# Graph convolution and mixture of experts on one core: blocks of 896 edges, the first norm on ScalarE, and a fixed order ahead of the gathers

## The chip, the core and the metric

The kernel runs on one core of one Trainium2 chip. The metric is device time in microseconds of one execution. Medians over several executions are compared; a profiled execution gives the trace. TensorE does matrix products, VectorE and ScalarE elementwise work[...], and SyncE (SP) and ScalarE issue plain transfers.

## The reference

`x` has 6250 rows of 256 numbers, and 106250 directed edges `src -> dst` are sorted by `dst`. Cut to what matters:

```python
def layernorm(x): return (x - mean(x)) / sqrt(var(x) + 1e-5)

def gnn(f, src, dst, W, b):
    ns = rsqrt(max(count(src), 1)); nd = rsqrt(max(count(dst), 1))
    msg = (f @ W)[src] * ns[src][:, None]
    return relu(segment_sum(msg, dst) * nd[:, None] + b)

def ffn(x):                       # 8 experts, hidden size 1024
    p = softmax(x @ Wr + br)      # the two best experts per row, weights renormed
    xn = layernorm(x)
    return sum over the 2 experts e of
        w_e * (gelu((xn * ln_g[e] + ln_b[e]) @ W1[e] + b1[e]) @ W2[e] + b2[e])

x = x + gnn(layernorm(x), src, dst, W, b)
x = x + ffn(layernorm(x))
```

## The kernel before

All work is in one function, `gnn_then_moe`. It has two stages, and the second interleaves three streams.

**Stage one, ahead of the gathers.** Rows are handled as 49 tiles of 128 (`NT`), in 7 groups of 7 (`NG`, `GT`). The stage prepares three things.

- *The counts of the source nodes.* Each index is split into its lower 7 bits and the rest (L272 to L278, `lo` and `hi`). The 831 columns of indices (`NCH`) go in 26 chunks of 32 (`GC`). For a chunk, function `count` compares the digits with a ramp on VectorE, giving two one-hot tensors, `oh_lo` (L340, 128x4096) and `oh_hi` (L345, 128x1568). TensorE then sums 32 products of them into `hist` (L350). The target nodes are counted in the same way into `hist_d`.
- *The edge blocks.* An edge list is laid out as rows of `BE` = 768 edges (`CE` = 6 columns of 128), 139 rows, so two partition groups (128 rows and 11). TensorE turns them so that an edge column lies along the partitions: `srcT` holds the sources, `relT` the targets relative to the block's window of 64 nodes (`WIN`). VectorE works out the windows, and counts the strays, the edges that fall outside; with none, a branch (L396) skips a repair part.
- *The table* `ytab` in HBM. A row is the normed row of `x` times `ns`, split into three bf16 pieces (`NPC`) whose sum is the fp32 value. The statistics come from VectorE (`stats`, L143 and L144). Per group VectorE makes `y` (L380), ScalarE rounds it to piece 1 (L385), VectorE subtracts (L386), ScalarE rounds piece 2 (L387), VectorE subtracts to piece 3 (L388), and SP stores the group (L389, 1344 KB). The tiles `y` and `yb` have two buffers each.

**Stage two.** A loop over the blocks, `for b in range(NBE)`. Per block POOL issues one indirect gather per column (L909, 128 table rows into `msg`, with `3 * CE` buffers), VectorE makes the one-hot `oh` of the targets (L915), TensorE sums the messages per node of the window (`pm`, L924), and VectorE adds this to `accT` at the window's place (L930). Beside the first 17 blocks (`HISTB`) go the chunks of `hist_d` that are not counted yet. When the last block that can touch a tile has gone (`CLOSE`), `tile_sums` makes its rows; after 9, 17, 25, 33, 40, 45 and 49 tiles `route_group` picks experts and POOL scatters the rows by expert (L688). Expert steps (`expert_step`, 56 of 256 rows, L845 and L858) run between the blocks, and POOL adds their results to the output (L867).

**Order.** The instructions of each engine come from a scheduler that may move work ahead of its place in the program. In the kernel before it puts 11 of the 26 chunks of `hist_d` among the work of stage one, ahead of the first gather. Each engine then runs its list strictly in order, and waits on semaphores.

Of the kernel before, what the change touches and what calls it, by code (L numbers as in the profile page):

```python
# [17 lines left out]
P = 128  # L18
# [4 lines left out]
def gnn_then_moe(  # L23
# [34 lines left out]
    CE = 6  # L58
# [3 lines left out]
    NCOL = NBE * CE  # L62
    WIN = 64
# [82 lines left out]

# [3 lines left out]
    NR = (P, NBE - P)  # L150
    dst_f = [early.tile([n, BE], F32, name=f"dst_f{h}") for h, n in enumerate(NR)]
    bad = [early.tile([n, BE], F32, name=f"bad{h}") for h, n in enumerate(NR)]
    flag_i = early.tile([1, 1], I32, name="flag_i")
    lo = {n: hl.tile([P, NCH], BF16, name=f"{n}_lo") for n in ("src", "dst")}
# [7 lines left out]
    scale = early.tile([P, NT], F32, name="scale")  # L162
    mv = early.tile([P, NT, 2], F32, name="mv")

    with tc.tile_pool(name="rows", bufs=1) as rows, tc.tile_pool(
        name="rowsp", bufs=2, space=PSUM
    ) as rowsp:
        flat = {}
        rows_i = {}
        for name, v, pad in (("src", src, 0), ("dst", dst, NOWHERE)):  # L170
            f = rows.tile([P, NCH], I32, name=f"{name}_flat")
            nc.vector.memset(f[:, FULL:NCH], NPAD - 1)
            b = rows.tile([NR[1], BE], I32, name=f"{name}_b")
            nc.vector.memset(b, pad)
            a = rows.tile([P, BE], I32, name=f"{name}_a")
            flat[name] = f
            rows_i[name] = (a, b)

        for name, v in (("src", src), ("dst", dst)):
            f, (a, b) = flat[name], rows_i[name]  # L180
            nc.sync.dma_start(f[:, :FULL], v[: FULL * P].rearrange("(p c) -> p c", p=P))
            if REST:
                nc.sync.dma_start(
                    f[:REST, FULL:NCH], v[FULL * P :].rearrange("(p c) -> p c", c=1)
                )
            nc.scalar.dma_start(a, v[: P * BE].rearrange("(p c) -> p c", p=P))
            nc.scalar.dma_start(
                b[: NR[1] - 1, :],
                v[P * BE : (NBE - 1) * BE].rearrange("(p c) -> p c", c=BE),
            )  # L190
            nc.scalar.dma_start(
                b[NR[1] - 1 : NR[1], :LASTE],
                v[(NBE - 1) * BE :].rearrange("(p c) -> p c", p=1),
            )

# [7 lines left out]
        for r0, r1 in ((0, split), (split, LASTROWS)):  # L203
# [3 lines left out]
        nc.scalar.dma_start(gw_sb, gnn_w.rearrange("(k p) d -> p k d", p=P))  # L207
        nc.scalar.dma_start(wr_sb, wr.rearrange("(k p) e -> p k e", p=P))
        nc.scalar.dma_start(b2_sb, b2)
        nc.scalar.dma_start(  # L210
            gb_sb, bass.AP(tensor=gnn_b.tensor, offset=gnn_b.offset, ap=[[0, P], [1, D]])
        )
        nc.scalar.dma_start(
# [3 lines left out]
        ident = const.tile([P, P], F32, name="ident")  # L217
        make_identity(nc, ident)
# [4 lines left out]
        nc.gpsimd.memset(accT, 0.0)  # L223
        nc.gpsimd.iota(iota_w, pattern=[[0, CE], [1, WIN]], base=0, channel_multiplier=0,
                       allow_small_or_imprecise_dtypes=True)
        ones = const.tile([P, P], F32, name="ones")
        nc.vector.memset(ones, 1.0)
# [6 lines left out]
        pcol = const.tile([P, 1], F32, name="pcol")  # L234
        nc.gpsimd.iota(pcol, pattern=[[0, 1]], base=0, channel_multiplier=1,
                       allow_small_or_imprecise_dtypes=True)
        eps = const.tile([P, 1], F32, name="eps")
        nc.vector.memset(eps, EPS)
        dump_xs = const.tile([P, 2], F32, name="dump_xs")
        dump_out = const.tile([P, 2], F32, name="dump_out")  # L240
        for s in range(2):
            nc.vector.tensor_scalar(
                dump_xs[:, s : s + 1], pcol, float(GONE + s * P), None, op0=ALU.add
            )
            nc.vector.tensor_scalar(
                dump_out[:, s : s + 1], pcol, float(N + 1 + s * P), None, op0=ALU.add
            )
# [12 lines left out]
        zeros = const.tile([P, SB * XW], F32, name="zeros")  # L260
        nc.vector.memset(zeros, 0.0)
        valid = const.tile([P, 1], F32, name="valid")
        nc.vector.tensor_scalar(valid, pcol, float(LASTROWS), None, op0=ALU.is_lt)

        accf = accT.rearrange("p k n -> p (k n)")
# [4 lines left out]
        for name in ("src", "dst"):  # L270
            part_i = rows.tile([P, NCH], I32, tag="part_i", name="part_i")
            nc.vector.tensor_scalar(part_i, flat[name], P - 1, None, op0=ALU.bitwise_and)  # L272
            nc.vector.tensor_copy(lo[name], part_i)
            part_j = rows.tile([P, NCH], I32, tag="part_i", name="part_j")
            nc.vector.tensor_scalar(
                part_j, flat[name], 7, None, op0=ALU.logical_shift_right
            )
            nc.vector.tensor_copy(hi[name], part_j)  # L278


        strays = rows.tile([P, 2, 2], F32, name="strays")
        nc.vector.memset(strays, 0.0)
        wrow = rowsp.tile([1, 2, P], F32, tag="wrow", name="wrow")
        for h in range(2):
            n = NR[h]
            s_f = rows.tile([n, BE], F32, tag="s_f", name="s_f")
            nc.gpsimd.tensor_copy(s_f, rows_i["src"][h])
            nc.gpsimd.tensor_copy(dst_f[h], rows_i["dst"][h])
            w_f = rows.tile([n, 1], F32, tag="w_f", name="w_f")
            nc.vector.tensor_scalar(  # L290
                w_f, dst_f[h][:, 0:1], float(NPAD - WIN), None, op0=ALU.min
            )
            rel = rows.tile([n, BE], F32, tag="rel", name="rel")
            nc.vector.tensor_scalar(rel, dst_f[h], w_f, None, op0=ALU.subtract)

            early_b = rows.tile([n, 1], F32, tag="early_b", name="early_b")
            nc.vector.tensor_scalar(
                early_b, pcol[:n], STEPN, STEPN * h * P - SLACK, op0=ALU.mult, op1=ALU.add
            )
            real = rows.tile([n, BE], F32, tag="real", name="real")  # L300
            nc.vector.tensor_scalar(
                real, dst_f[h], early_b, -100000.0, op0=ALU.is_lt, op1=ALU.mult
            )
            nc.vector.tensor_tensor(rel, rel, real, ALU.add)
            nc.vector.tensor_scalar(real, dst_f[h], 0.0, None, op0=ALU.is_ge)
            nc.vector.scalar_tensor_tensor(
                bad[h], rel, 0.0, real, op0=ALU.is_lt, op1=ALU.mult,
                accum_out=strays[:n, h, 0:1],
            )
            nc.vector.scalar_tensor_tensor(  # L310
                real, rel, float(WIN), real, op0=ALU.is_ge, op1=ALU.mult,
                accum_out=strays[:n, h, 1:2],
            )
            nc.vector.tensor_tensor(bad[h], bad[h], real, ALU.add)
            nc.tensor.transpose(wrow[:, h, :n], w_f, ident[:n, :n])
            nc.vector.tensor_copy(win_i[:, h * P : h * P + n], wrow[:, h, :n])
            b0 = h * P
            for v, vT in ((s_f, srcT), (rel, relT)):
                vT3 = vT.rearrange("p (b j) -> p j b", j=CE)
                for j0 in range(0, CE, 3):  # L320
                    pt = rowsp.tile([P, 3, P], F32, tag="ptE", name="ptE")
                    for j in range(j0, j0 + 3):
                        nc.tensor.transpose(
                            pt[:, j - j0, :n], v[:, j * P : (j + 1) * P], ident[:n, :n]
                        )
                    nc.vector.tensor_copy(
                        vT3[:, j0 : j0 + 3, b0 : b0 + n], pt[:, :, :n]
                    )
        total = rowsp.tile([P, 4], F32, tag="total", name="total")
        nc.tensor.matmul(  # L330
            total, ones, strays.rearrange("p a b -> p (a b)"), start=True, stop=True
        )
        flag_f = rows.tile([P, 1], F32, name="flag_f")
        nc.vector.tensor_reduce(flag_f, total, AX.X, ALU.add)
        nc.vector.tensor_copy(flag_i, flag_f[0:1, :])

    def count(pool, hist, name, c0):
        n = min(GC, NCH - c0)
        oh_lo = pool.tile([P, P, GC], BF16, tag="oh_lo", name="oh_lo")
        nc.vector.tensor_tensor(  # L340
            oh_lo[:, :, :n], iota_lo[:, :, :n],
            lo[name][:, None, c0 : c0 + n].to_broadcast([P, P, n]), ALU.is_equal,
        )
        oh_hi = pool.tile([P, NT, GC], BF16, tag="oh_hi", name="oh_hi")
        nc.vector.tensor_tensor(  # L345
# [10 lines left out]
    with tc.tile_pool(name="s1o", bufs=2) as s1o, tc.tile_pool(  # L356
# [4 lines left out]
        for g in range(NG):  # L361
            upto = (g + 1) * len(starts) // NG
            for c0 in starts[done:upto]:
                count(s1o, hist, "src", c0)
# [667 lines left out]
```

## Time and profile before

| what | value |
|---|---|
| median of 3 runs | 2113.53 us (2109.73 to 2114.85) |
| the profiled execution | 2114.36 us |
| its span on the core | 2112.4 us |
| first gather starts | 226.2 us into the span |
| first scatter by expert (L688) | 520.5 us |
| POOL busy, whole span | 1130.6 us (54%) |
| VectorE busy, whole span | 722.1 us (34%) |
| ScalarE busy, whole span | 328.3 us (16%) |

The span is what the trace covers; the 2.0 us between it and the profiled execution's own time lie around it. A row of the profile such as `L340 DVE TENSOR_TENSOR oh_lo<-iota_lo,src_lo 128x4096` names line, engine (DVE is VectorE, ACT ScalarE, PE TensorE), operation, result and inputs, then the count, the busy time, the mean ns of one, and the idle time of the engine just before with what ended it. In the page's strip of 40 slices one slice is 52.8 us, and a digit is the busy share in tenths.

### The profile page before, as it was taken

The numbers are of one execution on the slowest core, as the hardware profiler recorded it, in microseconds if no ns is written. First come the engines' busy times: TensorE is split into PE (matmuls) and PEld (weight loads), VectorE is DVE, ScalarE is ACT, GpSimd is POOL, SyncE is SP. The second block draws the span as 40 slices with busy tenths as digits, with TensorE's granted clock in tenths as the row PEclk, the third lists the DMA queues.
The fourth block names the chain that finished last, engine by engine and source line by source line (L and its number), as shares of the span: only waits on it lengthen the run. The fifth ranks groups of instructions, "written<-read, shape, count | busy, mean of one in ns | idle before, by whom it ended". The sixth has DMA issues, their size and how long they took to land.

```text
span 2112.4 us, 28889 instructions
## 1 busy us (share of the span) xinstructions
PE 1506.4 (71%) x11167; PEld 1236.4 (59%) x11167; DVE 722.1 (34%) x2078; ACT 328.3 (16%) x671; POOL 1130.6 (54%) x1065
## 2 busy tenths in 40 slices
PE   2872655656544659865899559985698678699998
PEld 1872544534433448754687437864487467488886
DVE  9999533324111412223222232323213422211111
ACT  0004000002100212112112022211121113122222
POOL 4000577777577756777377772777547731221222
PEclk9999999955655569975899659995699589799999
DMA  5004344556355567856577565865676653655654
GB/s 167 1 1 154 121 134 131 159 162 198 100 161 159 164 201 255 256 151 201 188 245 235 151 197 189 276 191 153 217 221 186 202 164 102 210 173 177 187 166 108
DMA packets 127309, 359.70 MB, mean 170 GB/s; under 512 B 21060, under 2 KB 75148, under 8 KB 120000
## 3 DMA queue, kind: packets, MB, share of 16 engines
q0 software_dynamic: 74208, 191.76, 33.6%
q1 hardware_dynamic: 51780, 164.79, 22.1%
q8 instruction: 89, 1.46, 0.3%
q10 hardware_dynamic: 1180, 1.26, 0.2%
q14 instruction: 52, 0.43, 0.1%
HBM read 311.58 MB, written 46.16 MB: 169 GB/s over the span
## 4 chain that ended last, share of the span: by engine, by line
PE 42%; DMA 23%; issue 10%; POOL 9%; DVE 3%; ACT 2%; SPq 0%; POOLq 0%; DVEq 0%; ACTq 0%
DMA msg<-ytab,srcT 17%; PE py L858 16%; PE ph L845 15%; POOL msg L909 6%; PE pm L924 5%; DMA xin<-xs 4%; POOL xs L688 2%; DMA xs<-rowt,pos_i 1%; PE pa L528 1%; PE pa L780 1%; PE pb L571 1%; DMA out_x<-yo,to_i 1%; PE ptf L829 1%; DVE yo L863 1%; PE pb L566 1%
## 5 line engine op out<-in xcount | busy, mean ns | idle before, releaser
L909 POOL DMA_INDIRECT msg<-ytab,srcT x834 | 833.2, 999 | 516.4 <-DVE oh L915 193.4
L924 PE MATMUL pm<-oh,msg 128*128 128x64 bf16 x5004 | 308.2, 219 | 292.9 <-DMA msg<-ytab,srcT 279.3
L924 PEld LDWEIGHTS <-msg 128*128 128x128 bf16 x5004 | 250.9, 114 | 368.8 <-DMA msg<-ytab,srcT 338.3
L858 PE MATMUL py<-w,hT 128*128 128x256 f32 x1792 | 421.0, 389 | 16.6 <-DVE yo L863 14.1
L845 PE MATMUL ph<-xeT,w 128*128 128x256 f32 x1792 | 412.6, 387 | 2.6 <-ACT hT L849 1.4
L867 POOL DMA_INDIRECT out_x<-yo,to_i x112 | 178.9, 1597 | 407.9 <-DVE yo L863 379.5
L858 PEld LDWEIGHTS py<-w,hT 128*128 128x128 f32 x1792 | 342.5, 194 | 70.2 <-DVE yo L863 23.3
L845 PEld LDWEIGHTS ph<-xeT,w 128*128 128x128 f32 x1792 | 327.7, 193 | 66.1 <-ACT hT L849 7.3
L849 ACT ACTIVATE hT<-ph,w 128x256 f32<-128x256 f32 x448 | 210.9, 473 | 759.6 <-PE ph L845 754.6
L350 PEld LDWEIGHTS <-oh_lo 128*128 128x128 bf16 x1662 | 164.8, 150 | 64.9 <-issue 55.8
L930 DVE TENSOR_TENSOR accT<-accT,pm 128x128 f32 x139 | 39.6, 285 | 344.6 <-PE pm L924 343.8
L812 DVE SCALAR_TENSOR_TENSOR to<-xin,dump_out 128x2 f32<-128x2 f32 x56 | 8.9, 159 | 415.4 <-DMA xin<-xs 415.4
L863 DVE TENSOR_SCALAR yo<-py,gate 128x256 f32<-128x256 f32 x112 | 54.1, 483 | 267.4 <-PE py L858 267.3
L350 PE MATMUL hist_d<-oh_hi,oh_lo 128*128 128x49 bf16 x831 | 89.4, 277 | 47.5 <-DVE oh_hi L345 47.0
L688 POOL DMA_INDIRECT xs<-rowt,pos_i x98 | 94.7, 966 | 41.9 <-issue 27.2
L528 PE MATMUL pa<-gw_sb,accT 128*128 128x256 f32 x196 | 73.5, 511 | 36.8 <-DVE keep L782 32.9
L350 PE MATMUL hist<-oh_hi,oh_lo 128*128 128x49 bf16 x831 | 84.7, 278 | 14.2 <-DVE oh_hi L345 13.6
L915 DVE TENSOR_TENSOR oh<-iota_w,relT 128x384 bf16<-128x384 bf16 x139 | 76.5, 554 | 26.5 <-PE pm L924 14.3
L829 PE MATMUL ptf<-ident,xin 128*128 128x128 f32 x224 | 37.9, 294 | 63.4 <-DMA xin<-xs 63.4
L780 PE MATMUL pa<-b_sb,wT 8*128 8x256 f32 x98 | 59.5, 708 | 26.7 <-DVE keep L782 23.2
L528 PEld LDWEIGHTS pa<-gw_sb,accT 128*128 128x128 f32 x196 | 45.1, 251 | 48.6 <-DVE keep L782 36.9
L829 PEld LDWEIGHTS ptf<-ident,xin 128*128 128x128 f32 x224 | 28.8, 150 | 73.1 <-DMA xin<-xs 67.4
(189 smaller groups left out, 990.9 us busy)
## 6 DMA issues: line engine op xcount, KB each, us to landing
w<-in_wcat SPq DMA_DIRECT2D x56, 2054.0 KB, 9.6
xin<-xs SPq DMA_DIRECT2D x56, 260.0 KB, 9.1
msg<-ytab,srcT POOLq DMA_INDIRECT x834
ytab<-yb SPq DMA_DIRECT2D x7, 1344.0 KB, 4.8
x_t<-in_x SPq DMA_DIRECT2D x48, 128.0 KB, 2.4
out_x<-keep SPq DMA_DIRECT2D x48, 128.0 KB, 3.0
xres<-in_x SPq DMA_DIRECT2D x6, 896.0 KB, 9.7
xs<-zeros SPq DMA_DIRECT2D x9, 260.0 KB, 2.3
```

The lines of the kernel that those rows point to most:

```text
L350: nc.tensor.matmul(hist, oh_lo[:, :, c], oh_hi[:, :, c], start=(c0 + c == 0), stop=(c0 + c == NCH - 1),)
L528: nc.tensor.matmul(pw, accT[:, k, t * P : (t + 1) * P], gw_sb[:, k, :], start=(k == 0), stop=(k == KD - 1),)
L688: sc = nc.gpsimd.indirect_dma_start(out=xs, out_offset=bass.IndirectOffsetOnAxis(ap=pos_i[:, j : j + 1], axis=0), in_=rowt[:, i, :], in_of ...
L780: nc.tensor.matmul(pb, wT, b2_sb, start=True, stop=True)
L829: nc.tensor.transpose(pt[:, k, s * P : (s + 1) * P], xin[:, s, k * P : (k + 1) * P], ident)
L845: nc.tensor.matmul(ph[:, c % 2, :], w[:, k * H + c * P : k * H + (c + 1) * P], xeT[:, k, :], start=(k == 0), stop=(k == KD - 1),)
L849: nc.scalar.activation(hT[:, c, :], ph[:, c % 2, :], AF.Gelu, bias=w[:, OB1 + c : OB1 + c + 1])
L858: nc.tensor.matmul(py[:, s, :], hT[:, c, s * P : (s + 1) * P], w[:, OW2 + c * D : OW2 + (c + 1) * D], start=(c == 0), stop=(c == HC - 1),)
L867: ad = nc.gpsimd.indirect_dma_start(out=out, out_offset=bass.IndirectOffsetOnAxis(ap=to_i[:, s : s + 1], axis=0), in_=yo[:, s, :], in_offs ...
L909: nc.gpsimd.indirect_dma_start(out=msg, out_offset=None, in_=ytab, in_offset=bass.IndirectOffsetOnAxis(ap=srcT[:, c : c + 1], axis=0),)
L915: nc.vector.tensor_tensor(oh, iota_w, relT[:, b * CE : (b + 1) * CE, None].to_broadcast([P, CE, WIN]), ALU.is_equal,)
L924: nc.tensor.matmul(pm[:, k, :], msgs[j][:, q * D + k * P : q * D + (k + 1) * P], oh[:, j, :], start=(j == 0 and q == 0), stop=(j == CE - 1 ...
```

## The change

- `CE` goes from 6 to 7: blocks of 896 edges, 119 of them, which fit into one partition group. There are 833 gathers (834 before), and 21 buffers of `msg` (18 before). The steps between the blocks are handed out over 17 to 23 blocks per group of tiles in place of 20 to 27.
- VectorE and ScalarE follow the program's own order in stage one (`manual_schedule`). All 26 chunks of `hist_d` and the digits of the targets now come after the branch, beside the gathers.
- The first norm goes to ScalarE: a sum per tile (49 ACTIVATEs with `accum_out`), a sum of squares per tile (49 more), and 49 in-place ACTIVATEs that norm `xres`. The source counts run beside it on VectorE and TensorE, in parts of 2, 9, 9 and 6 chunks.
- ScalarE also copies the turned edge columns out of PSUM (`turn`).
- `accT` is cleared by three VectorE memsets and five ScalarE copies, not by one POOL memset.
- Piece 1 is made per tile on ScalarE (`xres` times `ns`, rounded); VectorE makes the remainder `y` in one instruction per tile. Piece 2 is rounded by ScalarE in even groups and by VectorE in odd ones. Piece 3 and the store of a group come one group later in the program.
- The stray test is shorter (clamp, compare, count), and with the small constants is spread over the first four groups of the table (`the_rest`).
- Five loads of weights move from ScalarE's queue to SP's, behind those of `x`; the plain load of the targets also goes behind `x`.

The diff, cut to its core:

```diff
-    CE = 6
+    CE = 7
...
+    with tc.manual_schedule(
+        engines={mybir.EngineType.DVE, mybir.EngineType.Activation}
+    ), ...
...
-        nc.gpsimd.memset(accT, 0.0)
+        HEAD = 3072
+        for c0 in range(0, HEAD, 1024):
+            nc.vector.memset(accf[:, c0 : c0 + 1024], 0.0)
+        for c0 in range(HEAD, KD * NPAD, 2048):
+            n = min(2048, KD * NPAD - c0)
+            nc.scalar.copy(accf[:, c0 : c0 + n], zeros[:, 0:1].to_broadcast([P, n]))
...
+        digits(rows, "src", False)
...
+        counts(2)
+        for t in range(NT):
+            nc.scalar.activation(junk, xres[:, t, :], AF.Identity,
+                                 accum_out=sums[:, t : t + 1])
+        counts(9)
+        nc.vector.tensor_scalar(mean_n, sums, -1.0 / D, None, op0=ALU.mult)
+        for t in range(NT):
+            nc.scalar.activation(junk, xres[:, t, :], AF.Square, bias=mean_n[:, t : t + 1],
+                                 accum_out=sqs[:, t : t + 1])
+        nc.scalar.activation(sqs, sqs, AF.Sqrt, bias=eps, scale=1.0 / D)
+        turn(s_f, srcP)
...
+        turn(rel, relP)
+        counts(9)
+        nc.vector.reciprocal(rs0, sqs)
+        nc.vector.tensor_tensor(shift0, mean_n, rs0, ALU.mult)
+        for t in range(NT):
+            nc.scalar.activation(xres[:, t, :], xres[:, t, :], AF.Identity,
+                                 bias=shift0[:, t : t + 1], scale=rs0[:, t : t + 1])
+        counts(len(starts))
+        nc.vector.tensor_scalar(deg, hist, 1.0, None, op0=ALU.max)
+        nc.scalar.activation(nsd, deg, AF.Sqrt)
...
+        nc.vector.reciprocal(ns, nsd)
...
+            for g in range(NG + 1):
+                if g < NG:
+                    y = ys_[g] = s1y.tile([P, GT, D], F32, tag="y", name="y")
+                    yb = ybs[g] = s1y.tile([P, GT, NPC * D], BF16, tag="yb", name="yb")
+                    for i in range(GT):
+                        nc.scalar.activation(yb[:, i, :D], xres[:, t, :], AF.Copy,
+                                             scale=ns[:, t : t + 1])
+                    for i in range(GT):
+                        nc.vector.scalar_tensor_tensor(
+                            y[:, i, :], xres[:, t, :], ns[:, t : t + 1], yb[:, i, :D],
+                            op0=ALU.mult, op1=ALU.subtract)
+                    if g % 2 == 0:
+                        nc.scalar.copy(yb[:, :, D : 2 * D], y)
+                    else:
+                        nc.vector.tensor_copy(yb[:, :, D : 2 * D], y)
+                    the_rest(g)
+                if g:
+                    y, yb = ys_[g - 1], ybs[g - 1]
+                    nc.vector.tensor_tensor(
+                        yb[:, :, 2 * D :], y, yb[:, :, D : 2 * D], ALU.subtract)
+                    nc.sync.dma_start(ytab[...], yb)
...
     hist_d = dhp.tile([P, NT], F32, name="hist_d")
+    digits(cnt_pool, "dst", True)
```

`turn(v, to)` is seven transposes of 128 edge columns on TensorE into two PSUM tiles and two ScalarE copies out of them; both of its calls use the same two PSUM buffers. `counts(n)` calls `count` for the next `n` chunks of the sources.

## The prediction

> **What bounds the kernel now.** I read the page's strips first: they tell which stage has which limit. A slice is 52.8 us.
>
> ```profile
> DVE  9999533324111412223222232323213422211111
> ACT  0004000002100212112112022211121113122222
> POOL 4000577777577756777377772777547731221222
> ```
>
> For four slices VectorE is full, ScalarE nearly empty, and POOL idle after its first work: nothing is gathered. From slice 5 POOL is at 7 and VectorE falls to 3. So the first 226 us are VectorE's, and after that POOL matters. Second, the groups of the first 280 us, keeping shapes apart (busy us, mean ns, then idle):
>
> ```profile
> L350 PE MATMUL hist<-oh_hi,oh_lo 128*128 128x49 bf16 x831 | 84.7, 278 | 14.2 <-DVE oh_hi L345 13.6
> L340 DVE TENSOR_TENSOR oh_lo<-iota_lo,src_lo 128x4096 bf16<-128x4096 bf16 x25 | 56.7, 2269 | 4.1 <-PE hist L350 4.0 <-DVE flag_i L335 0.2
> L345 DVE TENSOR_TENSOR oh_hi<-iota_hi,src_hi 128x1568 bf16<-128x1568 bf16 x25 | 24.0, 960 | 0.0
> L143 DVE BATCH_NORM_STATS2 bnst<-xres 128x6 f32<-128x256 f32 x49 | 18.1, 406 | 0.0
> L386 DVE TENSOR_TENSOR y<-y,yb 128x1792 f32<-128x1792 f32 x7 | 14.2, 2024 | 0.0
> L272 DVE TENSOR_SCALAR part_i<-src_flat 128x831 int32<-128x831 int32 x1 | 12.6, 12554 | 1.9 <-DMA src_flat<-in_src 1.9
> L223 POOL MEMSET accT<- 128x12544 f32 x1 | 10.5, 10541 | 0.0
> ```
>
> A chunk of counts takes VectorE 3.1 us and TensorE 84.7/26 = 3.26 us: as soon as VectorE has nothing but counts, TensorE paces them. The 12.55 us of L272 stand beside POOL's memset; its twin L275 takes 0.59 us. Third, the timeline at the first gathers (start, duration), and fourth, L909 alone in windows of 25 us (busy, count, clock, DMA share, GB/s):
>
> ```profile
> 226.17 1.37 POOL L909 DMA_INDIRECT msg<-ytab,srcT  x1 [193.43 <-DVE oh L915]
> 227.84 3.08 POOL L909 DMA_INDIRECT msg<-ytab,srcT  x1 [0.30 <-issue]
> 231.22 0.95 POOL L909 DMA_INDIRECT msg<-ytab,srcT  x1 [0.30 <-issue]
> ```
>
> ```profile
> 300.00:325.00 25.00, 19.82 (x18) 1.00 0.47 134
> 350.00:375.00 25.00, 20.12 (x17) 1.00 0.42 120
> 450.00:475.00 25.00, 18.90 (x21) 0.50 0.55 159
> ```
>
> POOL never waits long here, yet it fits 17 or 18 gathers into 25 us while counts run, and 21 afterwards.
>
> **What the Trainium skill says, and whether this trace agrees.** (1) "ScalarE: Activation LUTs", section "What ACT_TABLE_LOAD costs": an ACTIVATE takes 186 ns + 0.833 ns per element, each per-partition pointer 93 ns more, and neighbours overlap by about 93 ns. L581 (256 elements, two pointers) gives 186 + 213 + 186 = 585; the trace has 592 alone, and 25.8/49 = 0.526 us in a row. The table load is 1.28 us in both. (2) "SBUF — State Buffer", section "SBUF: two separate sides": VectorE and GpSimd share a port pair under an exclusive lock. The 12.55 us of L272, and gathers of 3.08 us beside `oh_lo` against 0.95 us, agree. (3) "VectorE: DVE Perf Modes", section "The perf-mode tier table": an fp32 copy in SBUF runs at two elements a cycle, an fp32 two-tensor operation at one. L386 (2.02 us for 1792) agrees with the latter. From the former I estimate 1.1 us for the new rounding of piece 2 on VectorE, which no run here shows yet.
>
> **The change part by part.** Times are from the span's start.
>
> *Start of the counts.* The POOL memset goes, so the digits wait only for the ramp `iota_lo` (4.2 us, over at 7) and VectorE's memsets (three of 1024 elements, about 1.0 us each by L261's 0.49 us for 520). Digits 0.6 to 1.1 us each, so ready at about 11; a chunk is 3.1 us, so TensorE starts counting at 14 (before: source counts at 53, behind two chunks of targets at 46.5). ScalarE's share of clearing `accT` is 9472 elements x 0.833 ns + 5 x 0.1 us = 8.5 us, from 5 to 14 behind its four transfers; `x` has landed by about 25 (DMA is full in 10:30).
>
> *The norm on ScalarE.* Sum: 399 ns (no pointer). Square: 492 ns (one pointer; L849 shows 473). All 98 write the same `junk`, so they don't overlap. The accumulator's cost on ScalarE is in no row: below 0 is excluded, as work is only added; the upper end is a whole small instruction (L778, 0.25 us); VectorE's accumulator read beside L306 takes 0.08 us. I take 0.1 us for this with the wait between them: 0.50 and 0.60 us. Sums 14 + 24.5 = 38.5. VectorE reaches the mean after 11 chunks, at 14 + 10 x 3.26 = 46.6; squares to 76; table load and root 1.6 us; 77.6. TensorE has 616 products ahead of the transposes of `rel`, so is there at 14 + 616 x 0.102 = 77, and waits for ScalarE to copy `srcT` out of the two PSUM tiles: 1 to 2 us, with the chunks queued behind it. Copies and transposes end at 80, then 49 norms x 0.526 = 25.8 us: 106; `ns` at **107**. TensorE ends at 80 + 215 x 0.102 = 102, so ScalarE decides. At 0.25 us for the accumulator `ns` is at 118; at 0 it is 103.
>
> *The table.* VectorE alone would need 7 x (7 x 0.35 + 2.0) + 3 x 1.1 = 34 us (`y` at L380's streaming pace, one subtraction like L388, three roundings). But the subtraction and store of group g-1 now stand behind piece 1 and `y` of group g, and `yb` has two buffers: piece 1 of group g+1 waits for the store of g-1. That closes a loop: subtraction 2.0, issue 0.2, store 4.8 (section 6 of the page), seven ACTIVATEs with one pointer 2.9, the last `y` 0.5, and in odd groups 1.1: 10.4 or 11.5 us per group. From `ns`: first subtraction at 14.6 (piece 1 twice, 3.7 each, piece 2, `y`, `the_rest` 2.0), five turns of 55, two subtractions: 72. Before, the last subtraction ended at 217.5 and the first gather came 8.7 us later (store, branch, `oh`); two stores now end close together, so 10. First gather at 107 + 72 + 10 = **189**, against 226.2: **-37 us**. Bounds 182 to 202.
>
> *Removed from VectorE and not to be seen in full:* statistics 26 us, stray chains some 14 us, 11 chunks of targets 34 us, the wait on POOL 12 us. Of these 86 us only 37 come out at the first gather: behind them the ScalarE chain (norms to 106) and the store loop are late next.
>
> *Moved behind the gathers.* From 226.2 to 400 before, 15 + 104 = 119 gathers took 173.8 us; at the 1.255 us of the later windows they would take 149.3. The 24.5 us are 15 chunks of targets: 1.63 us each. Now 26 chunks and the four instructions of the target digits (3 us on VectorE, 2 taken) lie there: 26 x 1.63 + 2 = 44.4: **+20 us**. POOL is in line without a gap up to the first scatter (520.5), so this goes straight to the end of that stage. On VectorE a chunk now stands behind its block's addition (L930), which waits for TensorE; per block TensorE has 42 x 0.064 + 1.5 x 3.26 = 7.6 us and POOL 7 x 1.255 + 1.5 x 1.63 = 11.2, so neither holds POOL up. The last chunk comes at 189 + 119 x 1.255 + 44 = 382 us, and 392 before (L939). A chunk can't cost less than 0 nor more than the 3.1 us that VectorE holds it.
>
> *Blocks of seven.* Gathers and products are the same (833 and 4998, before 834 and 5004). Twenty blocks less save 20 x (0.55 + 0.29) us of VectorE, which has room, less the wider `oh`. Three more buffers let POOL be ahead by 3 x 1.255 us at each of the five later routes: -19 at best; three expert parts per block at first, not two, can make a gather wait: +10 at worst. I take **-3**. Loads moved to SP's queue, behind `x`, are needed from tile 0 on (after 380) and cost nothing; SP's first store is at about 120, when they have long landed. If `x` were late, sums would start late: they have 8 us of slack. The new code of the repair isn't entered.
>
> *Sum.* -37 + 20 - 3 = -20 us: span 2092.4, own time 2114.4 - 20 = 2094.4; the median shown is 0.8 lower: **2094 us**.
>
> **Rivals.** (A) *The counts hide:* 11 more chunks cost POOL nothing, as their cost turns up as slack later. Against it: the gathers never pause before 520. For it: POOL does pause later (busy 20 of 50 us in 1000:1050). 2094 - 18 = 2076. (B) *A longer ScalarE chain:* at 0.35 us per accumulating ACTIVATE the 98 add some 20 us, TensorE stands at the transposes of `rel`, and VectorE with it; 2114, no change. (C) *Denser counts hold POOL longer* (slower). In the first 17 blocks there are 1.5 chunks per 7 gathers, before under 1 per 6, so two chunks in a row can hold the port pair, and POOL finds no gap. At 2.4 us per chunk the gain is gone (26 x 2.4 + 2 - 24.5 = 40 = 37 + 3); from 2.65 it is slower; at 2.8, 2094 + 26 x 1.17 = 2124. For it: single gathers of 3.08 and 2.71 us. Against it: the mean so far is 1.63.
>
> **How the numbers follow.** A measurement tells about 0.3% (6.3 us) from no change. The forecast 0.55 (its own range 2081 to 2107), A 0.18, B 0.12, C 0.15. Faster: nearly all of the forecast, A, and a little of B: 0.74; same 0.12; slower 0.14. The range 2070 to 2118 takes in A and B and half of C.
>
> **What would show it.** Right: first gather at 182 to 202; `ns` at 103 to 118; stores about 11 us apart with ScalarE's piece 1 waiting on the store; about 1.6 us of POOL time per chunk; the first scatter near 503. Wrong: a first gather under 175 (no store loop) or over 210 (ScalarE); gathers above 1.7 us on average in the first 17 blocks (C); a time from the first scatter to the end that differs from the 1592 us before by over 15 us.

## The result, and the profile after

The changed kernel takes **2118.01 us** (median of 12 runs, 2115.85 to 2121.7), the kernel before 2113.79 us (12 runs). The ratio is 1.0022, 95% interval 1.0013 to 1.0031: no change by the 0.3% that such a measurement tells apart, and if anything slower. The forecast was 20 us less. The profiled execution took 2116.38 us with a span of 2114.3 us, so by the traces it is 1.9 us longer than before, and the account below is made against these 1.9 us.

Some groups of runs further down were made on other chips, which granted TensorE a lower clock (0.76 to 0.81, against 0.82 to 0.83 here) and on which the kernel before takes 2358 to 2381 us, so a kernel is compared by its ratio to the kernel before on the same chip.

The strips of the changed kernel's page (40 slices of 52.9 us; POOL is GpSimd, and PEclk is the clock granted to TensorE in tenths):

```profile
DVE  7955445433212322224222232222312421211111
ACT  6952000002000212112121022211121122122222
POOL 2001788777577746777367773777537722221222
PEclk9999999955655579875799758995699589699999
```

ScalarE now works in the first four slices, and POOL starts its gathers half a slice earlier. After that the POOL row reads nearly as before. The groups of the stage ahead of the gathers, shapes kept apart (busy us, mean ns, then idle before):

```profile
L187 PE MATMUL hist<-oh_hi,oh_lo 128*128 128x49 bf16 x831 | 85.4, 279 | 3.0 <-DVE oh_lo L182 2.5
...
L182 DVE TENSOR_TENSOR oh_lo<-iota_lo,src_lo 128x4096 bf16<-128x4096 bf16 x25 | 57.1, 2286 | 0.0
L323 ACT ACTIVATE junk<-xres,mean_n 128x256 f32<-128x256 f32 x49 | 25.3, 517 | 6.1 <-DVE mean_n L321 4.5
...
L318 ACT ACTIVATE junk<-xres 128x256 f32<-128x256 f32 x49 | 20.9, 426 | 1.5
L420 ACT ACTIVATE yb<-xres,ns 128x256 bf16<-128x256 f32 x49 | 20.3, 494 | 43.2 <-DMA ytab<-yb 42.6 <-DVE ns L375 0.6
L424 DVE SCALAR_TENSOR_TENSOR y<-xres,ns,yb 128x256 f32<-128x256 f32 x49 | 20.1, 482 | 32.1 <-ACT yb L420 32.1
...
L318 ACT ACTIVATION_READ_ACCUMULATOR junk<-xres 128x1 f32 x49 | 9.2, 187 | 0.0
...
L431 DVE CAST yb<-y 128x1792 bf16<-128x1792 f32 x3 | 6.1, 2020 | 0.1
```

The statistics (L143) and the one slow digit instruction (L272) of before are gone. The costs are the same per chunk (L187, L182), but ScalarE stands 42.6 us at piece 1 (L420) until a store of `ytab` has landed, and VectorE 32.1 us behind it (L424). The first gathers, from the timeline of POOL, and the gathers alone in windows of 25 us (busy, count, clock, DMA share, GB/s):

```profile
201.31 1.27 POOL L964 DMA_INDIRECT msg<-ytab,srcT  x1 [166.31 <-DVE part L169]
202.88 2.63 POOL L964 DMA_INDIRECT msg<-ytab,srcT  x1 [0.30 <-issue]
```

```profile
226.00:251.00 25.00, 19.82 (x18) 1.00 0.48 134
351.00:376.00 25.00, 20.25 (x16) 1.00 0.45 124
451.00:476.00 25.00, 19.12 (x20) 0.50 0.57 160
```

The first gather is 24.9 us earlier (201.3 against 226.2). By the first scatter (514.6 against 520.5) 5.9 us of this are left, at the last gather 2.0 us (1704.3 against 1706.4), at the end less than nothing. The lead is lost in three places: 19 us beside the target counts, 4 us between the first scatter and the last gather, though that stretch has five gathers less, and 4 us after it.

What POOL waited for between the first scatter and the last gather, first the kernel before (520 to 1706 us), then the changed one (514 to 1704 us); the columns are the sum, the times, and the longest:

```profile
POOL msg L909 <- PE pm L924: 93.6, 83, 12.7
POOL out_x L867 <- DVE yo L863: 87.1, 21, 9.1
```

```profile
POOL out_x L921 <- DVE yo L917: 100.1, 17, 15.7
POOL msg L964 <- PE pm L979: 97.4, 84, 11.8
```

In all, the waits for `pm` (a free `msg` buffer) grew by 4 us and those of `out_x`, POOL's adds of an expert's rows to the output, by 13 us. An add stands in POOL's list between the gathers: while it waits for its expert step, the gathers behind it wait too. But the sums hide where the loss lies. Between the first and the second scatter (a scatter here is that of one group of tiles) both kernels stand for about the same time: 24.0 us for `pm` before, now 18.4 us at two adds and 6.1 us for `pm`. From the second scatter to the third the changed kernel takes 263.4 us with 140 gathers, in place of 247.4 with 132, and from the third to the fourth 256.9 with 133 in place of 255.8 with 138. With 1.255 us taken off for each gather these two stretches are 5.9 and 7.3 us longer than before, and the others together 3.2 us shorter. POOL's waits from the second scatter to the third, before (743.5 to 990.9 us) and after (732.7 to 996.0 us):

```profile
POOL out_x L867 <- DVE yo L863: 18.3, 5, 8.8
POOL msg L909 <- PE pm L924: 16.0, 17, 7.1
```

```profile
POOL msg L964 <- PE pm L979: 25.0, 20, 11.0
POOL out_x L921 <- DVE yo L917: 16.5, 4, 8.8
```

It is the wait for a `msg` buffer that grew there, by 9.0 us, and by 7.7 us in the next stretch (15.1 to 22.8).

### The profile page after: what moved, and what is told of

It reads as the page before. It is cut to its first block, busy times and chain, and to the rows that moved or that the text cites. A ratio compares the mean times of both kernels' runs of the same rounds, so it can differ in the third digit from the quotient of the medians.

```text
span 2114.3 us, 28964 instructions
## 1 busy us (share of the span) xinstructions
PE 1495.9 (71%) x11150; PEld 1232.2 (58%) x11150; DVE 670.8 (32%) x1915; ACT 423.7 (20%) x963; POOL 1125.2 (53%) x1061
## 4 chain that ended last, share of the span: by engine, by line
PE 43%; DMA 21%; POOL 10%; issue 9%; DVE 4%; ACT 2%; SPq 0%; POOLq 0%; DVEq 0%; ACTq 0%
PE py L912 16%; PE ph L899 16%; DMA msg<-ytab,srcT 15%; POOL msg L964 7%; PE pm L979 5%; POOL xs L742 3%; DMA xin<-xs 3%; DMA out_x<-yo,to_i 2%; PE pa L834 2%; DMA xs<-rowt,pos_i 1%; PE pb L625 1%; PE pa L582 1%; PE pb L620 1%; DVE yo L917 1%; PE ptf L883 1%
## 5 line engine op out<-in xcount | busy, mean ns | idle before, releaser
L979 PE MATMUL pm<-oh,msg 128*128 128x64 bf16 x4998 | 292.1, 218 | 341.5 <-DMA msg<-ytab,srcT 259.5
L979 PEld LDWEIGHTS <-msg 128*128 128x128 bf16 x4998 | 245.1, 114 | 406.3 <-DMA msg<-ytab,srcT 309.6
L899 PE MATMUL ph<-xeT,w 128*128 128x256 f32 x1792 | 417.6, 390 | 1.9 <-DVE xeT L888 0.9
L187 PEld LDWEIGHTS <-oh_lo 128*128 128x128 bf16 x1662 | 163.8, 150 | 10.6 <-DVE oh_lo L182 9.6
L985 DVE TENSOR_TENSOR accT<-accT,pm 128x128 f32 x119 | 34.0, 286 | 300.2 <-PE pm L979 291.9
L187 PE MATMUL hist_d<-oh_hi,oh_lo 128*128 128x49 bf16 x831 | 86.2, 278 | 2.4 <-DVE oh_lo L182 2.4
L187 PE MATMUL hist<-oh_hi,oh_lo 128*128 128x49 bf16 x831 | 85.4, 279 | 3.0 <-DVE oh_lo L182 2.5
L970 DVE TENSOR_TENSOR oh<-iota_w,relT 128x448 bf16<-128x448 bf16 x119 | 73.9, 622 | 16.4 <-PE pm L979 9.1
```

What stands on the lines that cost most here:

```text
L187: nc.tensor.matmul(hist, oh_lo[:, :, c], oh_hi[:, :, c], start=(c0 + c == 0), stop=(c0 + c == NCH - 1),)
L899: nc.tensor.matmul(ph[:, c % 2, :], w[:, k * H + c * P : k * H + (c + 1) * P], xeT[:, k, :], start=(k == 0), stop=(k == KD - 1),)
L979: nc.tensor.matmul(pm[:, k, :], msgs[j][:, q * D + k * P : q * D + (k + 1) * P], oh[:, j, :], start=(j == 0 and q == 0), stop=(j == CE - 1 ...
```

## The experiments

**The start of the counts.** Edit to the changed kernel:

```diff
-            nc.scalar.dma_start(in_rows[name][: NBE - 1, :], ...)       # 118 partitions
+            nc.scalar.dma_start(in_rows[name][:112, :], ...)
+            nc.sync.dma_start(in_rows[name][112 : NBE - 1, :], ...)
```

> The changed kernel, with the two loads of edge rows (118 partitions each) cut into 112 partitions on ScalarE's queue and 6 on SP's. Theory (these transfers use few DMA engines, land at 18.6 and 30.3 us, and hold ScalarE's queue and TensorE's counts): src rows land by 10 us, TensorE counts from about 15 (now 21), ScalarE sums from about 16 (now 23.7, then paced by x), ns about 6 us earlier at 112, first gather 195; if a lead at the first gather passes to the end, total 2112. Rival (x sets the start, the row loads only take bandwidth from it): ns and first gather move by under 2 us, total 2118.

The timelines, first of the changed kernel in the pair (ScalarE with its queue; POOL), then of this run (POOL; SP's queue):

```profile
3.24 10.75 ACTq L226 DMA_DIRECT2D dst_rows<-in_dst  x1
14.02 1.28 ACT L292 ACT_TABLE_LOAD   x1 [14.02 <-DVE oh_hi L177]
15.31 8.52 ACT L292 COPY accT<-zeros 128x2048 f32<-128x2048 f32 x5
23.73 0.41 ACT L318 ACTIVATE junk<-xres 128x256 f32<-128x256 f32 x1
```

```profile
18.62 0.93 POOL L263 CAST s_f<-src_rows 119x896 f32<-119x896 int32 x1 [11.66 <-DMA src_rows<-in_src]
```

```profile
7.31 1.24 POOL L263 CAST s_f<-src_rows 119x896 f32<-119x896 int32 x1 [0.35 <-DVE eps L296]
```

```profile
3.28 15.17 SPq L233 DMA_DIRECT2D xres<-in_x  x7
```

In the changed kernel POOL waits 11.7 us for `src_rows`, TensorE has the turns of `s_f` ahead of its counts, and ScalarE's fourth transfer holds its sequencer for 10.75 us. With 112 partitions the rows are there at 7.3, TensorE counts from 14.1 (21.1 in the pair), ScalarE sums from 14.0 (23.7), piece 1 starts at 110.6 (118.3), and the first gather comes at 193.4, 7 to 8 us earlier (200.4 for the changed kernel on a chip with such a clock, 201.3 in the pair). Even the seven loads of `x` are issued in 15.2 us in place of 31.3. "The Trainium skill", page "DMA: Bandwidth & Descriptors", section "Why a DMA increments its semaphore by 16 and not by 1", says that a transfer uses the largest number of DMA engines up to 16 that divides the outer dimension of both its sides; for 118 that is 2, for 112 it is 16. The landing times agree; the engines themselves were not counted. The ratio, 1.0006 (0.9981 to 1.0031), beside 1.0043 for the changed kernel in a group of such a clock (below), does not resolve 8 us.

**The store loop.** Edit to the changed kernel: `yb` in a pool of its own with three buffers (and `s_f` and `rel` in one tile, for the space).

```diff
-        with tc.tile_pool(name="s1y", bufs=2, side="right") as s1y:
+        with tc.tile_pool(name="s1y", bufs=2, ...) as s1y, tc.tile_pool(name="s1yb", bufs=3, ...) as s1yb:
```

> The changed kernel with three buffers of yb in place of two (s_f and rel share one tile to make room). Theory (the store loop costs the table: piece 1 waits for the store of two groups before): ScalarE no longer waits on ytab, the table takes about 52 us from ns in place of 74, first gather near 180; if the later stages pass a lead on one to one, total 2097. Rival 1 (the lead is absorbed later, since something other than the gathers paces the middle): first gather near 180, total above 2108. Rival 2 (VectorE or the stores pace the table anyway): first gather not before 195.

Piece 1 in the timeline of ScalarE, changed kernel, then this run:

```profile
137.07 2.90 ACT L420 ACTIVATE yb<-xres,ns 128x256 bf16<-128x256 f32 x7 [10.88 <-DMA ytab<-yb]
...
147.99 2.10 ACT L420 ACTIVATE yb<-xres,ns 128x256 bf16<-128x256 f32 x5 [5.79 <-DMA ytab<-yb]
```

```profile
137.25 2.90 ACT L420 ACTIVATE yb<-xres,ns 128x256 bf16<-128x256 f32 x7 [0.66 <-DMA ytab<-yb]
142.38 2.90 ACT L420 ACTIVATE yb<-xres,ns 128x256 bf16<-128x256 f32 x7 [2.23 <-DMA ytab<-yb]
```

A turn shrinks from 11 to 13 us to about 5 to 8 us, and the first gather comes at 174.2: 26 us earlier than at 200.4. The ratio is 0.9917 (0.9892 to 0.9943), 1.3% under the 1.0043 of the changed kernel. So at this clock an earlier first gather does pass to the end, and neither rival holds. The lead was not absorbed by something that paces the middle anyway; it was lost to something added.

**The block size, and how expert parts are handed out.** First the kernel before with `CE = 7` alone (its two partition groups become 96 and 23 rows), run twice.

> The kernel before with blocks of 896 edges and nothing else changed (119 blocks, 833 gathers, 21 msg buffers; the front still works in two partition groups, of 96 and 23 rows). Theory (the block size is what gives the lead back: the prediction's term 'Blocks of seven' is -3, the traces suggest +10 to +13): first gather within 4 us of the kernel before (226), the time from first scatter to the end about 12 us longer than 1592, total about 2124 us (ratio 1.005). Rival (the term is right, the lead is lost because of the counts or of an engine that paces the middle of the kernel): total 2111 us or less, from first scatter to the end 1585 to 1592.

Ratio 1.0115 (1.0085 to 1.0145), more than the theory's 1.005.

> The kernel before with blocks of 896 edges and nothing else changed, once more, to be had at the granted clock of the pair (0.82). Theory (the block size with the old hand-out costs 10 to 13 us there): ratio 1.004 to 1.007. Rival (the term was -3): ratio 0.997 to 1.0.

The second time the clock was 0.79 in place of the pair's 0.82: ratio 1.0143 (1.0098 to 1.0187). Blocks of 896 cost over 1% there; the rival of -3 us is out at that clock. At the pair's clock this kernel was not measured.

The suspect was the hand-out of expert parts. By the constants in the kernel a group's parts are handed out over 8 to 20 blocks (10 to 23 before), not over the 17 to 23 of the section on the change. The hand-out rounds up. After the second and third scatter the changed kernel so starts with three parts per block, the kernel before with two; after the fourth both start with three, after the fifth and sixth with four and three. The stretches after the second and third scatter are those in which the pair lost its 5.9 and 7.3 us. Four in place of three after the fifth cost nothing that the pair shows (-1.1 us). Rounded down, the changed kernel starts with two (three after the fifth and sixth scatter), the kernel before with one or two, and the larger parts come last. First the changed kernel, then the kernel before with either block size:

```diff
-            for _ in range(-(-left // blocks)):
+            for _ in range(left // blocks):
```

> The changed kernel, but the expert parts of a group are handed out low first: two per block and then three (three or four at first in the changed kernel). Theory (three parts in a row on TensorE after a route keep the gathers' products waiting, POOL finds no free msg buffer; this is what blocks of seven cost): POOL's gaps after the second and third scatter shrink by about 5 us each, total 2106. Rival (the size of a block itself, seven products released at once, is the cause; or the number of parts does not matter): gaps within 2 us of the changed kernel, total 2116 to 2120.

Ratio 0.9849 (0.9818 to 0.9881).

> The changed kernel with the low-first hand-out alone, at the pair's clock. Theory (the hand-out gives back the lead): ratio 0.988 to 0.994. Rival (at this clock low-first alone does nothing, only the hold does): 1.000 to 1.003.

Ratio 0.9877 (0.9841 to 0.9913), again at the lower clock.

> The kernel before (blocks of 768 edges) with only the hand-out of expert parts changed: low first (one or two per block, the rest later). Theory (three parts in a row on TensorE are the harm, and blocks of 768 start with two): little to gain, ratio 0.997 to 1.0. Rival (fewer parts at first help any kernel, since POOL catches up after a route): ratio 0.985 to 0.99.

Ratio 0.9895 (0.9855 to 0.9935): as the rival said. The kernel before gains too, about 1%.

> The kernel before with blocks of 896 edges and the low-first hand-out. Theory (the hand-out is what the larger block costs): the same as the kernel before with low-first hand-out, within 0.2%. Rival (the size of the block costs by itself): over 0.5% longer than that one.

Ratio 0.9921 (0.9886 to 0.9955): within 0.3% of the smaller blocks, and the intervals overlap. With the old hand-out the same two kernels are 1.2 to 1.4% apart. Between first scatter and last gather the `out_x` waits are 169.3 us in the second run of blocks of 896 and 124.1 us here; the `pm` waits are 199.9 and 188.8 us. So at this clock most of what the block size costs comes through the hand-out. The edit does two things that these runs don't separate: besides the three parts in a row, it moves the one expert step of the first group, whose first add stands 3 gathers behind the first scatter in the changed kernel and 73 behind it with the hand-out rounded down (4 and 78 in the kernel before).

> The changed kernel itself, unchanged, beside the next three on one chip, since the four runs before these had a lower granted clock (0.77) than the pair of the result (0.82). Expected: ratio to the kernel before 1.002 if the clock is as in the pair, 1.004 to 1.010 if it is 0.77 again.

The changed kernel at that lower clock has 1.0043 (1.0019 to 1.0066), 1.7 to 1.9% above the same kernel with the hand-out rounded down.

Then both kernels with the hand-out rounded down and nothing handed out for the first two blocks after a route. This group of runs had the pair's level again (the kernel before 2114.83 us).

```diff
-        if work is not None:
+        if work is not None and b > held:
...
-                        left = steps[0] * 5 + 1
+                        left, held = steps[0] * 5 + 1, b + 2
```

> The changed kernel with the new hand-out only (low first, and nothing for the first two blocks after a route); its front is as it was. Theory (an earlier first gather passes to the end whatever the hand-out): the two front edits bring some 29 us, so this one is 1.2 to 1.5% longer than the run with all edits: ratio 0.966 to 0.970. Rival (the front edits are worth less once POOL waits less): ratio 0.960 or less.

> The kernel before with the same new hand-out only. Theory (with the hand-out mended, the changed kernel keeps what its first gather gains, 25 us less the counts' cost of 10 to 14): ratio 0.971 to 0.978, 0.5% longer than the changed kernel with this hand-out. Rival (blocks of 768 need no mending beyond low first, or the gain of the front is lost elsewhere): the same as the changed kernel with this hand-out, or shorter.

Changed kernel: 2053.49 us, ratio 0.9706 (0.9690 to 0.9721). Kernel before: 2075.19 us, 0.9816 (0.9802 to 0.9829). Both are above their theories (0.966 to 0.970 and 0.971 to 0.978), the first by little. With this rule of handing out for both, the change is worth 21.7 us. It is luck that this is close to the forecast of 20: the traces make it of -25.8 us at the first gather, +19.2 up to the first scatter, -16.0 up to the last gather and +4.1 to the end, where the forecast had -37, +20 and -3. Nor is the hand-out quite the same, since two blocks are 14 gathers in one kernel and 12 in the other. POOL's waits in the stretch from first scatter to last gather, first the changed kernel with this hand-out (514 to 1642 us), then the kernel before with it (521 to 1665 us):

```profile
POOL msg L964 <- PE pm L979: 100.4, 75, 12.3
...
POOL out_x L921 <- DVE yo L917: 22.8, 7, 9.3
```

```profile
POOL msg L909 <- PE pm L924: 96.0, 84, 12.2
POOL out_x L867 <- DVE yo L863: 45.6, 13, 8.8
```

The waits for `pm` stay where they were, 96 to 100 us. The waits of `out_x` fall from 100.1 to 22.8 and from 87.1 to 45.6 us, and the stretch is 62 and 42 us shorter than in the pair. The granted clock in it is higher too (0.78 against 0.75 for the changed kernel), but TensorE's busy time there fell by 16 us only, from 837.4 to 821.1, so the clock alone does not make the 62 us. What rounding down and the hold do of this, each by itself, was not measured at this level. What such waits look like in the timelines of the changed kernel of the pair, after its second scatter: POOL from 779 us on, and TensorE over the same time.

```profile
779.62 1.56 POOL L921 DMA_INDIRECT out_x<-yo,to_i  x1 [2.70 <-DVE yo L917]
790.00 1.55 POOL L921 DMA_INDIRECT out_x<-yo,to_i  x1 [8.82 <-DVE yo L917]
794.30 1.55 POOL L921 DMA_INDIRECT out_x<-yo,to_i  x1 [2.75 <-DVE yo L917]
804.36 1.02 POOL L964 DMA_INDIRECT msg<-ytab,srcT  x1 [8.51 <-PE pm L979]
```

```profile
778.66 7.09 PE L899 MATMUL ph<-xeT,w 128*128 128x256 f32 x32
785.58 3.62 PE L912 MATMUL py<-w,hT 128*128 128x256 f32 x16
789.04 0.60 PE L883 MATMUL ptf<-ident,xin 128*128 128x128 f32 x4
789.47 0.31 PE L979 MATMUL pm<-oh,msg 128*128 128x64 bf16 x5
789.78 3.72 PE L912 MATMUL py<-w,hT 128*128 128x256 f32 x16
793.34 7.09 PE L899 MATMUL ph<-xeT,w 128*128 128x256 f32 x32
800.26 3.62 PE L912 MATMUL py<-w,hT 128*128 128x256 f32 x16
803.71 0.66 PE L979 MATMUL pm<-oh,msg 128*128 128x64 bf16 x17
```

From 778.7 to 803.7 us TensorE runs expert parts with only five products of gathers among them. At 790.0 POOL has stood 8.8 us in front of an expert step's add, with gathers queued behind it, and at 804.4 it has stood 8.5 us for a free `msg` buffer. The kernel before has the same wait of 8.8 us at an add in this stretch; its longest wait for a buffer there is 7.1 us, against this one and one of 11.0 us.

> The kernel before with blocks of 896 edges, low-first hand-out and the hold of two blocks. Theory (with the hand-out mended, the block size costs nothing): the same as the kernel before with that hand-out, ratio 0.979 to 0.983. Rival (the block size costs by itself): 0.986 or more.

Ratio 0.9810 (0.9767 to 0.9853) for the kernel before with blocks of 896 and this hand-out, against 0.9816 with blocks of 768 in the group above. The two groups differ in clock, so this comparison is a weak one; but like the pair of runs with low-first hand-out alone, which are on one chip and within 0.3%, it shows no cost of the block size by itself.

**Three more buffers.** The changed kernel with the hand-out rounded down, and `bufs=18` for `msg` in place of 21.

> The changed kernel with low-first hand-out and 18 msg buffers in place of 21. If three more buffers let POOL be ahead by 3 gathers at each route (the prediction's -19 at best): 10 to 19 us longer than with 21 buffers and low-first hand-out (ratio 0.985 there, so 0.989 to 0.993). Rival (buffers do not decide): ratio 0.983 to 0.987.

Ratio 0.9840 (0.9800 to 0.9880): the same as with 21 (0.9849 and 0.9877). At this clock the buffers do not decide, and nothing speaks for the -19 in the prediction's bounds.

**The counts beside the gathers.** The changed kernel without them, run twice, both times at a clock of 0.78 to 0.79:

```diff
-    digits(cnt_pool, "dst", True)
...
-                count(cnt_pool, hist_d, "dst", c0)
+                pass
...
-                nc.vector.tensor_scalar(deg_in, hist_d, 1.0, None, op0=ALU.max)
+                nc.vector.memset(deg_in, 17.0)
```

> The changed kernel without the target digits and the 26 chunks of target counts beside the gathers (left out: the target degree is a constant). The prediction's price is 1.63 us per chunk (44 us with the digits), the pair of traces suggests 1.4 (38 us). Theory (the counts lengthen the first stretch of gathers and that goes to the end): from first gather to first scatter 35 to 44 us less than the changed kernel, total 1.5 to 1.8% less than it. Rival (TensorE at half clock paces this stretch, the counts only fill gaps of POOL): under 15 us less.

> The changed kernel without the target digits and the 26 chunks of target counts (left out: the target degree is a constant), once more, at the pair's clock. Theory (1.4 us per chunk plus the digits, and it goes to the end): first gather to first scatter 36 to 40 us less than the 313 of the changed kernel, ratio 0.984 to 0.988. Rival (part of it is hidden, as it was at the lower clock): 15 to 25 us less, ratio 0.990 to 0.994.

Ratios 0.9921 (0.9888 to 0.9954) and 0.9949 (0.9924 to 0.9975). From first gather to first scatter it took 326.5 and 322.0 us, against 345.2 us with the counts (`f4_after_again`) and, on the chip of the second run, 346.2 us (`m3_after_low`): 19 and 24 us less. The first lies between its theory and its rival, the second in its rival's range. On these chips the gathers are slower even without counts (17 to 19 in most windows of 25 us, against 20 in the pair after its counts), so part of the counts' cost can be hidden there. The clock alone is not the reason: in the second run it was 1.00 from 226 to 351 us, and TensorE was busy for 43 of these 125 us. The price on the pair's chip was not measured by leaving the counts out.

**All together.** The three edits in one kernel, then with the hold of two blocks, then with a hold of four (`held = b + 4`).

> The changed kernel with three edits: row loads of 112 and 6 partitions, three buffers of yb, low-first hand-out. If their effects add (first gather 8 + 22 us earlier, hand-out some 1%): first gather near 171, ratio 0.972 to 0.980 to the kernel before. If one hides the other: ratio 0.983 or more.

> The changed kernel with the three edits of the run before (row loads, three yb, low-first hand-out), and the expert parts of a group held back for the first two blocks after a route. Theory (after a route TensorE stands in order at the first expert's xin for some 6 to 12 us and then runs expert steps with no gathers' products between them, so POOL waits for msg buffers): POOL's waits on pm of some 11 and 8 us after each route shrink, ratio 0.955 to 0.965. Rival (the parts held back only pile up later): ratio 0.970 or more.

> The three edits and a hold of four blocks. If TensorE's run of expert parts after a route is all that is left to gain: ratio under 0.950. If the parts then pile up before the next route (three and four per block): 0.954 or more.

Ratios 0.9704 (0.9653 to 0.9754), 0.9540 (0.9505 to 0.9576), and 0.9424 (0.9408 to 0.9441). The first gathers are at 166.2 to 166.5 us. The gains add up or better, and nothing of the hold of four is lost again to parts that pile up. The last kernel takes **1993.93 us**, beside 2114.83 us for the kernel before on the same chip, and beats both kernels by over 5%. A hold of two with the other edits was run in another group than the hold of four; but the changed kernel with the hold of two above is of the same group as the last kernel. From first scatter to last gather, where the two edits of the front don't reach, it takes 1127.9 us, and the last kernel 1101.9: the longer hold is worth 26 us. By this, an estimate, the 2 gathers by which the hold of the changed kernel is longer than that of the kernel before are worth some 4 of the 21.7 us.

## Why the prediction failed, step by step

The prediction had -37 + 20 - 3 = -20 us. The traces have -24.9 at the first gather, +19.0 up to the first scatter (of it 5.0 for four more gathers that lie there: 214 in place of 210, at 1.255 us), +3.9 up to the last gather with 619 gathers in place of 624 (so 10.1 us apart from the gathers), and +4.0 from there to the end. The sum is +2.0, and the spans differ by 1.9.

*Start of the counts: wrong by 7 us.* "TensorE starts at 14" took no account of the row loads, which the change made from 128 into 118 partitions. TensorE started at 21.1, and at 14.1 as soon as they were cut at 112.

*The norm on ScalarE: the chain right, ends late.* The accumulator's cost was taken as 0.1 us. It is a read of its own of 0.187 us, overlapped in part: a sum takes 0.545 us and a square 0.64 us, where 0.50 and 0.60 were used. Squares began at 55.0 (46.6 predicted: the late counts), the root was done at 87.9 (77.6), and the copies of `rel` took 3.7 us, so the norms began at 93.1 (80). ScalarE went to piece 1 at 118.3, behind `ns` (107 predicted, bounds 103 to 118). About 8 of the 11 us came from the start.

*The table: the loop right, the sum in part by luck.* The last subtraction ended 74 us after `ns` (72 predicted; the prediction's own parts, 14.6, 55 and two subtractions of 2.0, make 73.6), the first gather 9.1 us later (10). The loop through the two `yb` buffers was as described, and a third buffer took 27 us of it away. Two errors cancelled: the first subtraction came 11.5 us after `ns`, not 14.6, and the five turns took 58.5 us, not 55. One estimate in it failed: the rounding of piece 2 on VectorE takes 2.02 us (L431), not the 1.1 us worked out from "VectorE: DVE Perf Modes", section "The perf-mode tier table"; this copy, which writes bf16 into seven separate runs of 256 in rows of 768, takes as long as the subtraction of as many elements before (L386). Whether the type or the seven runs do it was not tested.

*Moved behind the gathers: the total about right, the base wrong.* The 214 gathers at 1.255 us are 268.6 us of the 313.3, so counts and digits cost 44.7 us (44.4 predicted). That leans on the price of a gather: the 79 that start between 400 and 500 us have a mean pace of 1.27 us, which would make it 41. But the prediction took 119 gathers from adding seven windows for the kernel before, and a gather that lies across a border counts in both. By start times there are 116 up to 400 us, so the 15 chunks cost 28 us there, not 24.5. Net, the traces show +14 where it had +20.

*Blocks of seven: wrong, and the largest part of the miss.* Of the 22 us between -20 and +2, 12 are at the first gather, 13 are here, 4 come after the last gather, and -6 are beside the counts; one gather less makes the rest. So this is the step that failed most: -3 was predicted, with +10 "at worst" because "three expert parts per block at first, not two, can make a gather wait". The traces show that worst case: +10 up to the last gather, all of it in the two stretches in which three parts per block replace two (+5.9 and +7.3), with longer waits for `pm` there (16.0 to 25.0 and 15.1 to 22.8 us). The mechanism was named, and the -19 of the three more buffers was set against it; but at the lower clock 18 buffers did as well as 21, and with the hand-out mended blocks of 896 cost no more than blocks of 768. That it is the rounding at the pair's clock too rests on where the loss lies in its traces; the block size alone was not run there. After the last gather the traces have +4, which the prediction did not have. It is +4.1 again with the mended hand-out in both kernels, so the rounding and the hold do not make it; its cause is open. What the prediction left out altogether are POOL's adds, behind which the gathers queue: they are not why the changed kernel is slower than the one before, but most of what the new hand-out then gained.

*The rivals.* (A) is out: the counts' cost did not turn up as slack. (B) had about the right number, no change, for part of a reason: ScalarE's chain was 11 us late, half of what it asks, and most of that from the late start, not from the accumulator. (C) is out, at 1.7 us per chunk with the digits counted in. None had the loss after the first scatter, and the test that the text gave for it (over 15 us in the time from first scatter to the end) was set too wide: that time grew by 7.8 us, with 5 gathers less in it.

## What to carry to other kernels

Changing a block size also changes every rounding that is done per block: count the parts handed out per block, and look in the profile for what waits in the in-order list of the engine that carries the main stream; here full `msg` buffers, and adds whose results were not there yet, held POOL's gathers. Give late-needed work (experts just routed) a delay of some blocks, so that its inputs and outputs are ready when their instructions come up. Split a wait by stages before naming it: over the whole stretch the adds seemed to have grown, and stage by stage it was the buffers. A lead won at the start passes to the end only as far as no such wait is added on the way; measure it at each milestone, not in the total alone.

## What the runs showed of the hardware beyond what was expected

- Two loads of 413 KB with 118 partitions took until 18.6 and 30.3 us and slowed the loads of `x` beside them from 15.2 to 31.3 us of issue; with 112 + 6 partitions they were there at about 7 and 10 us.
- An ACTIVATE with an accumulator is followed by a record of its own of 0.187 us, of which some 0.12 us add to the pace (0.545 us for 256 elements where the ACTIVATE alone is 0.426).
- ScalarE's copy of 476 elements from PSUM took 0.99 us into int32 (`srcT`) and 2.17 us into bf16 at the same stride of seven elements (`relT`).
- In the runs on the chips with the lower clock TensorE stood 134 to 264 us ahead of `pm` for nothing that the profile shows ("issue"), in up to 348 places. In the runs at the pair's level it stood there for 204 to 280 us until gathers had landed, and on those chips only 42 to 114 us for that. So it may be one and the same wait, which the profile names in one case and not in the other; this is open.
